# Graph attention and routed experts on one core: sends in every planner step, and the setup in short parts on three engines

## The chip, the core and the metric

The kernel runs on one NeuronCore of a Trainium2 chip. The core has TensorE (PE, matrix products; PEld is its weight load), VectorE (DVE), ScalarE (ACT), GpSimd (POOL) and SyncE (SP, which issues most of the DMAs). Each engine works through its own instructions in the order in which the program lists them, and waits at an instruction until what that one needs is there. The metric is the device time of one execution in microseconds, the median of the runs.

## The reference

The input `x` holds 64 batches of 256 rows with 256 features. Two layers follow each other. Each is an attention over a fixed graph of 256 nodes and then a per-row network, both added to the row.

```python
x = x + _L0_gnn_ref(_layernorm(x), adj, L0_gnn_W, L0_gnn_a)            # 4 heads of 64, elu
x = x + _L0_ffn_ref(_layernorm(x), L0_ffn_weight, L0_ffn_bias)          # one 256x256 linear layer
x = x + _L1_gnn_ref(_layernorm(x), adj, L1_gnn_W, L1_gnn_a)            # 1 head of 256, relu
x = x + _L1_ffn_ref(_layernorm(x), router_w, w1, b1, w2, b2)            # 8 experts, the best 2 per row
```

The attention: `h = x @ W`; `e[i,j] = leaky(h[i].a_src + h[j].a_dst)`, masked by `adj`; the output is `softmax(e) @ h`. The experts: `logits = tokens @ router_w.T`; the two largest per row get softmax weights; the output is `tokens + sum over the two of weight * (gelu(tokens @ w1[e]) @ w2[e] + b2[e])`. All of it is float32.

## The kernel before

**Tiles.** A batch is two tiles of 128 rows. The layers of one batch are one Python generator, `batch_layers` (line 485), that emits a stretch of instructions, yields a rank, and goes on in the next step: transposed input (116), statistics of the rows (353 to 362, the last two on GpSimd), projection `pq` (384), its exponentials (392) and scaling (400), the scores `z` (454, 461), `pv` (475), the linear layer `pf` (529), the second attention (419, 443, 475, 551), the normed rows `xng` and the residual `base` (569, 574), and the router logits (599).

**Planner.** The loop at line 1059 runs in steps. In each step every active generator is advanced once, by rising rank; the order in which instructions are emitted is the order in which each engine runs them. Three steps make a tick (`TICKS`), and `phase = step % 3`. One batch begins in each tick, at phase 2.

**Routed experts.** The first 62 batches are routed. They form chunks (`CHUNKS`: twelve of four batches, six of two, two of one). When a chunk has its logits, `route` (907) picks the two experts per row, counts positions with two small products (924, 925), computes the destinations, and then sends each row, by indirect DMAs from GpSimd (`send`, 888), to an area `xs` in device memory that is sorted by expert. A chunk of four batches has eight groups of two sends, one group at a time with a `yield` between. `later(rank, phases)` (901) yields until the step has one of the given phases. When all are sent, the pairs of 128-row tiles that are now full are appended to `waiting`, together with the names of the chunk's sends, on which the pairs' loads must wait (`needs`).

**Pairs.** `expert_pair` (710) handles one pair of 128 rows for one expert: loads `xr`, `xt` (726, 737) and the expert's weights `we` (752) by SP, a transposition on DVE (757), the two products `ph` (784) and `py` (799), the result `y` on DVE (809), its scaling on ACT (777), and two scattering indirect DMAs from GpSimd that add into `out` (`scatter`, 814). There are 131 pairs. Each scatter waits until both scatters of the pair before have landed (`before = added[-2:]`), since rows may repeat from pair to pair. Results have nine buffers. The planner begins waiting pairs at phase 1, as far as `credit` reaches (1072): it grows by 2 a tick (by 3 from step 180 on, `DRAIN_AT`) and is capped at 3. From step 209 on (`QUIET`) it begins one a step. One scatter is emitted per step. Batches 62 and 63 are not routed: all eight experts run on them (`dense_expert`, 836).

**Setup.** Before the first batch the kernel loads `adj`, makes the first mask (`fill_mask`, 145, on DVE and PE), and prepares the first layer's weights (`gnn_weights`, `score_columns`, `center`): four products and four reductions on DVE give the columns for the scores, and the columns' means are subtracted. Four more preparations, `prepare_f`, `prepare1`, the second mask and `prepare_r`, are jobs of one step each, begun one a step from step 3 on, and after them eight jobs that pack the experts' weights. Their DVE instructions stand between those of the first batches.

Of the kernel before, what the change touches and what calls it, by code (L numbers as in the profile page):

```python
# [27 lines left out]
def kernel(  # L28
# [102 lines left out]
    ones = const.tile([P, P], F32, tag="ones", name="ones")  # L131
# [3 lines left out]
    mhalf = const.tile([P, 2 * NT], F32, tag="mhalf", name="mhalf")  # L135
    nc.vector.memset(mhalf, -0.5)

    adj_i = work.tile([P, NT, N], adj.dtype, tag="z", name="adj_i", bufs=6)
    nc.scalar.dma_start(out=adj_i, in_=adj.rearrange("(t p) j -> p t j", p=P))

    masks = [
        const.tile([P, NT, N], F32, tag=f"mask{layer}", name=f"mask{layer}") for layer in range(2)
    ]

    def fill_mask(layer, op):
        mf = work.tile([P, NT, N], F32, tag="xT", name=f"maskf{layer}", bufs=4)
        nc.vector.tensor_scalar(mf, adj_i, 0.0, None, op0=op)
        pm = bank("pm", [NT, N])
        for t in range(NT):
            for j in range(NT):  # L150
                nc.tensor.transpose(
                    pm[:, j, t * P : (t + 1) * P], mf[:, t, j * P : (j + 1) * P], ident
                )
        nc.vector.tensor_copy(masks[layer], pm)

    fill_mask(0, ALU.is_gt)

    def center(w, cols):


        pc = bank("pc", [cols])
        for k in range(KT):
            nc.tensor.matmul(pc, mean_w, w[:, k, :], start=(k == 0), stop=(k == KT - 1))
        for k in range(KT):
            nc.vector.tensor_sub(w[:, k, :], w[:, k, :], pc)

    def gnn_weights(w, a, heads, slope, name):

        rows = lambda w, k: (
            w.rearrange("(p k) o -> k p o", k=KT) if heads > 1
            else w.rearrange("(k p) o -> k p o", k=KT)
        )[k]
        d = D // heads
        wx = const.tile([P, KT, heads, d + 3], F32, tag=name, name=name)  # L180
        for k in range(KT):
            nc.sync.dma_start(
                out=wx[:, k, :, :d],
                in_=rows(w, k).rearrange("p (h d) -> p h d", h=heads),
            )
        av = work.tile([P, 2, d], F32, tag="e", name=name + "_a", bufs=1)
        nc.scalar.dma_start(out=av.rearrange("p s d -> p (s d)"), in_=rows_to_all(a, 2 * d))
        flat = wx.rearrange("p k h c -> p k (h c)")
        return flat, lambda: score_columns(wx, av, heads, slope, name)

    def score_columns(wx, av, heads, slope, name):
        d = D // heads
        flat = wx.rearrange("p k h c -> p k (h c)")
        prod = work.tile([P, heads, d], F32, tag="hp", name=name + "_p", bufs=1)
        for k in range(KT):
            for s, c in ((0, d + 1), (1, d)):
                nc.vector.tensor_mul(
                    prod, wx[:, k, :, :d], av[:, s : s + 1, :].to_broadcast([P, heads, d])
                )
                nc.vector.tensor_reduce(wx[:, k, :, c : c + 1], prod, AX.X, ALU.add)  # L200
            nc.vector.tensor_scalar(
                wx[:, k, :, d + 1 : d + 2], wx[:, k, :, d + 1 : d + 2], 1.0 - slope, None,
                op0=ALU.mult,
            )
            nc.vector.tensor_scalar(
                wx[:, k, :, d + 2 : d + 3], wx[:, k, :, d : d + 1], slope - 1.0, None,
                op0=ALU.mult,
            )
        center(flat, heads * (d + 3))

    wx0, prepare0 = gnn_weights(w0, a0, H, SLOPE0, "wx0")
    xblk = {0: load_blocks(0)}
    xin = {0: load_batch(0)}
    prepare0()
    wx1, prepare1 = gnn_weights(w1g, a1g, 1, SLOPE1, "wx1")

    wf_in = work.tile([P, KT, D], F32, tag="xT", name="wf_in", bufs=4)
# [3 lines left out]
    wfT = const.tile([P, KT, D], F32, tag="wfT", name="wfT")  # L221
# [3 lines left out]
    def prepare_f():  # L225
        pw = bank("pw", [KT, D])
        for t in range(KT):
            for k in range(KT):
                nc.tensor.transpose(
                    pw[:, k, t * P : (t + 1) * P], wf_in[:, t, k * P : (k + 1) * P], ident  # L230
                )
        nc.vector.tensor_copy(wfT, pw)
        center(wfT, D)

        nc.vector.tensor_scalar(bias_f, bias_f, -1.0, None, op0=ALU.add)

    r_in = work.tile([E, D], F32, tag="x1b", name="r_in", bufs=1)
    nc.scalar.dma_start(out=r_in, in_=router)
    rT = const.tile([P, KT, E], F32, tag="rT", name="rT")

# [58 lines left out]
    def once(work):  # L299
        work()  # L300
        return
        yield


    setup = [
        lambda work=work: once(work)
        for work in (prepare_f, prepare1, lambda: fill_mask(1, ALU.not_equal), prepare_r)
    ]
    setup += [lambda e=e: pack_expert(e) for e in range(E)] + [fill_spare]

# [590 lines left out]
    def later(rank, *phases):  # L901

        yield rank
        while more and order_steps[-1] % TICKS not in phases:
            yield rank

    def route(c, row0, nt, n, last, xng, lg):
# [11 lines left out]
        spread = nt == NTC  # L919
# [42 lines left out]
        if last:  # L962
            ends_at = rt([E], "ends_at", 2, I32)
            vec.tensor_copy(ends_at, rows[0])
        yield from later(95, 1, 2)
        mark = len(sent)
        for t in range(nt):
            for k in range(2):
                send(xng[t // NT][:, t % NT, :], pos[:, k, t : t + 1])
            if n and spread and t in (1, 3):  # L970
                ids, ef = next(parts) or (None, None)
            if not last:
                yield from later(95, 1, 2)
            elif t % 2:
                yield 95
        needs = sent[mark:]
# [77 lines left out]


    DRAIN_AT, QUIET = TICKS * (B - 4), TICKS * B + 17
    SETUP_AT = 3
    with tc.manual_schedule():
        while more or active or waiting or dense_jobs or scatters:
            phase = step % TICKS  # L1060
            if phase == 2 and more:
                nxt = next(batches, None)
                more = nxt is not None
                if more:
                    begin(nxt, 25)
            if step >= SETUP_AT and setup:
                begin(setup.pop(0)(), 90)
            if step >= QUIET:
                if waiting and len(scatters) < 3:
                    begin(waiting.pop(0)(), 90)  # L1070
            elif phase == 1:
                credit = min(credit + (2.0 if step < DRAIN_AT else 3.0), 3.0)
                while waiting and credit >= 1.0:
                    credit -= 1.0
                    begin(waiting.pop(0)(), 90)
            if dense_jobs and step % DENSE == 0:
                begin(dense_jobs.pop(0)(), 90)
# [54 lines left out]
```

## Time and profile before

| | |
|---|---|
| Median of 3 runs | 1650.05 us (1646.56 to 1652.72) |
| Profiled execution | 1651.53 us, of which the span that the profile covers is 1649.6 |
| Busy in the span | PE 1476.3 us (89%), PE weight load 1299.8, DVE 1323.8 (80%), ACT 831.0 (50%), POOL 889.4 (54%) |
| Mean granted PE clock | 0.955 |
| Scatters (line 820, POOL) | 262, 1585 ns each |
| Sends (line 890, POOL) | 248, 1012 ns each |
| Chain that ended last | PE 62%, DVE 21%, DMA 5%, POOL 4% |

A busy share is an average over the whole span. The parts of this kernel have different limits, so the prediction reads it in parts: the start, the ticks of the middle, and the end. In a row of a timeline the first number is the start in us from the beginning of the span, the second the duration; `[... <-X]` is the idle time of the engine before the instruction and what ended it.

### The profile page before, as it was taken

Reading aid. Unit: us, or ns where it says so; the run is one execution under the profiler, and the core shown is the slowest. Engines: PE = TensorE matmul, PEld = TensorE weight load, DVE = VectorE, ACT = ScalarE, POOL = GpSimd, SP = SyncE. Lnnn points to the kernel's source line nnn. Section 1 sums busy time; section 2 is a strip of 40 time slices with the busy share of each in tenths; the row PEclk is TensorE's granted clock in tenths of the full one; section 3 lists DMA queues with packets and bytes.
Section 4 is the critical chain, followed back from the end, with each engine's and each line's share of the span. In section 5 each row is a group of like instructions: output and inputs, shape, how many; then the busy total and the mean of one; then the engine's idle time right before and its main releaser. Section 6 shows DMA issues by size and latency. Waiting matters only on the chain.

```text
span 1649.6 us, 30216 instructions
## 1 busy us (share of the span) xinstructions
PE 1476.3 (89%) x8474; PEld 1299.8 (79%) x8474; DVE 1323.8 (80%) x4494; ACT 831.0 (50%) x1832; POOL 889.4 (54%) x853
## 2 busy tenths in 40 slices
PE   5898888999999999999999999999989997599930
PEld 4777777778888888888888888887878886488820
DVE  6888989999898989898989898999988877545510
ACT  0244344445666666565656666655555565343310
POOL 0121343444757575756575757566664677544444
PEclk8999999999999999999999999999999998799965
DMA  4812123254756565656666675756575667887633
GB/s 109 231 44 58 55 71 101 72 140 113 158 132 135 135 146 135 140 138 145 140 127 156 117 170 108 163 117 146 135 140 124 136 127 152 188 178 135 128 38 45
DMA packets 364132, 207.37 MB, mean 126 GB/s; under 512 B 264248, under 2 KB 334912, under 8 KB 363968
## 3 DMA queue, kind: packets, MB, share of 16 engines
q1 hardware_dynamic: 313344, 137.07, 33.7%
q0 software_dynamic: 49632, 67.39, 22.8%
q8 instruction: 70, 1.15, 0.3%
q10 hardware_dynamic: 992, 0.99, 0.2%
q14 instruction: 94, 0.77, 0.2%
HBM read 116.19 MB, written 89.15 MB: 124 GB/s over the span
## 4 chain that ended last, share of the span: by engine, by line
PE 62%; DVE 21%; DMA 5%; POOL 4%; issue 3%; ACT 3%; SPq 1%; DVEq 0%; POOLq 0%; ACTq 0%
PE pv L475 14%; PE ph L784 13%; PE py L799 12%; PE pq L384 5%; PE pq L419 5%; PE pf L529 4%; DVE z L461 3%; PE pt L368 3%; DVE stats L353 3%; DMA out_dram<-y,xt 3%; POOL out_dram L820 2%; PE pl L599 2%; DVE mv L354 2%; ACT xT L374 1%; PE pd L454 1%
## 5 line engine op out<-in xcount | busy, mean ns | idle before, releaser
L820 POOL DMA_INDIRECT out_dram<-y,xt x262 | 415.4, 1585 | 241.1 <-DMA out_dram<-y,xt 87.6
L475 PE MATMUL pv<-q,z 128*128 128x65 f32 (+1 forms) x2560 | 368.5, 299 | 3.7 <-DVE z L461 3.7
L475 PEld LDWEIGHTS pv<-q,z 128*128 128x128 f32 x2560 | 331.5, 194 | 15.5 <-DVE z L461 4.0
L361 POOL TENSOR_SCALAR rstd<-mv 128x4 f32<-128x4 f32 (+1 forms) x132 | 71.0, 538 | 432.2 <-DVE mv L354 337.1
L890 POOL DMA_INDIRECT xs<-xng,pos x248 | 250.9, 1012 | 68.8 <-issue 65.7
L799 PE MATMUL py<-w2s,hT 128*128 (+1 forms) x1176 | 266.1, 379 | 1.3 <-ACT hT L790 1.2
L784 PE MATMUL ph<-sT,we 128*128 128x256 f32 x1048 | 242.8, 385 | 11.8 <-DVE y L809 9.6
L799 PEld LDWEIGHTS py<-w2s,hT 128*128 128x128 f32 x1176 | 219.5, 190 | 30.0 <-ACT hT L790 2.2
L374 ACT COPY xT<-pt 128x512 f32<-128x512 f32 x192 | 113.3, 590 | 232.5 <-PE pt L368 232.4
L784 PEld LDWEIGHTS ph<-sT,we 128*128 128x128 f32 x1048 | 198.9, 194 | 38.5 <-issue 9.9
L461 DVE SCALAR_TENSOR_TENSOR z<-pd,q,mask 128x256 f32<-128x256 f32 x512 | 211.1, 473 | 0.3 <-PE pd L454 0.2
L790 ACT ACTIVATE hT<-ph,we 128x256 f32<-128x256 f32 x294 | 122.5, 472 | 126.2 <-PE ph L784 103.8
L362 POOL TENSOR_TENSOR rstd<-rstd,mhalf 128x4 f32<-128x4 f32 (+1 forms) x132 | 163.0, 1235 | 11.0
L777 ACT ACTIVATE y<-y,w 128x256 f32<-128x256 f32 x262 | 112.6, 501 | 100.1 <-DVE y L809 100.1
L353 DVE BATCH_NORM_STATS2 stats<-x 128x6 f32<-128x256 f32 x384 | 156.3, 407 | 2.2
L384 PE MATMUL pq<-wx,xT 128*128 128x268 f32 x512 | 139.2, 418 | 8.6 <-DVE wt L257 4.2
L419 PE MATMUL pq<-wx,xT 128*128 128x259 f32 x512 | 129.1, 394 | 15.6 <-ACT xT L374 15.6
L809 DVE TENSOR_TENSOR y<-py,b2s 128x512 f32<-128x512 f32 x131 | 85.8, 686 | 68.6 <-PE py L799 48.8
L384 PEld LDWEIGHTS pq<-wx,xT 128*128 128x128 f32 x512 | 101.8, 204 | 30.4 <-issue 6.9
L419 PEld LDWEIGHTS pq<-wx,xT 128*128 128x128 f32 x512 | 91.9, 189 | 42.0 <-ACT xT L374 30.7
L529 PE MATMUL pf<-wfT,xT 128*128 128x256 f32 x512 | 124.1, 386 | 0.0
L551 ACT ACTIVATE rel<-pv,rinv 128x256 f32<-128x256 f32 x128 | 53.9, 474 | 110.6 <-DVE rinv L482 110.5
(152 smaller groups left out, 2256.1 us busy)
## 6 DMA issues: line engine op xcount, KB each, us to landing
we<-wpack SPq DMA_DIRECT2D x139, 288.0 KB
xr<-xs SPq DMA_DIRECT2D x524, 64.0 KB
xblk<-in_x_dram SPq DMA_DIRECT2D x256, 64.0 KB
xin<-in_x_dram SPq DMA_DIRECT2D x64, 256.0 KB
out_dram<-base SPq DMA_DIRECT2D x64, 256.0 KB
out_dram<-y,xt POOLq DMA_INDIRECT x262, 3.9
xs<-xng,pos POOLq DMA_INDIRECT x248, 2.9
xs<-fill SPq DMA_DIRECT2D x9, 260.0 KB
```

Of the source, the lines that this page charges most:

```text
L353: nc.vector.bn_stats(stats[:, t, :], src[:, t, :])
L362: nc.gpsimd.tensor_tensor(rstd[:, :n], rstd[:, :n], mhalf[:, :n], ALU.pow)
L374: nc.scalar.copy(dst, pt)
L384: nc.tensor.matmul(pq.rearrange("p h c -> p (h c)"), xT[:, k, t * P : (t + 1) * P], wx[:, k, :], start=(k == 0), stop=(k == KT - 1),)
L419: nc.tensor.matmul(pq, xT[:, k, t * P : (t + 1) * P], wx1[:, k, :], start=(k == 0), stop=(k == KT - 1),)
L461: nc.vector.scalar_tensor_tensor(z[:, j, :], pd[:, i, :], q[:, j, h, d + 2 : d + 3], mask[:, j, :], op0=ALU.max, op1=ALU.mult,)
L475: nc.tensor.matmul(pv[:, h, :], z[:, j, t * P : (t + 1) * P], q[:, j, h, : d + 1], start=(j == 0), stop=(j == NT - 1),)
L529: nc.tensor.matmul(pf[:, t, :], xT[:, k, t * P : (t + 1) * P], wfT[:, k, :], start=(k == 0), stop=(k == KT - 1),)
L784: nc.tensor.matmul(ph[:, f, :], we[:, k * D + f * P : k * D + (f + 1) * P], xT[:, k, :], start=(k == 0), stop=(k == KT - 1),)
L799: nc.tensor.matmul(py[:, t, :], hT[:, f, t * P : (t + 1) * P], w2s[:, e, f * D : (f + 1) * D].rearrange("p e c -> p (e c)"), start=(f == 0 ...
L820: d = nc.gpsimd.indirect_dma_start(out=out_rows, out_offset=bass.IndirectOffsetOnAxis(ap=xt[:, t, 0:1].bitcast(I32), axis=0), in_=y[:, t, ...
L890: d = nc.gpsimd.indirect_dma_start(out=xs_d[: E * CAP * PAIR, :], out_offset=bass.IndirectOffsetOnAxis(ap=at, axis=0), in_=xe, in_offset=None,
```

## The change

It has four parts.

1. In `route`, the sends yield plainly: one group of two sends is emitted in every step, where `later` kept them to phases 1 and 2. The second half of the allotment of pairs (`next(parts)`) moves from the fourth group to the fifth, which is the same step as before.
2. The credit of pairs fills up in each tick to 2 (3 from `DRAIN_AT` on) and is no longer saved from one tick to the next.
3. The columns for the scores are made with fewer, wider instructions: the scores vector is scaled first, the products for the source and destination columns go to one tile, and one reduction takes both. Of the first layer's products one half is made by GpSimd, of the second layer's all. The copies of both masks and of `wfT` out of PSUM move from DVE to ACT. `adj` is loaded after the first scores vector instead of before it, and the first mask is made after the first layer's columns. A one-element exponential on ACT stands ahead of the rest and takes the table load.
4. The preparations are generators with a yield between their parts, so that a part is emitted per step; they begin at step 4, and with them the packing of the experts begins one step later. Some temporary tiles use other buffers.

```diff
-        nc.vector.tensor_copy(masks[layer], pm)
-
-    fill_mask(0, ALU.is_gt)
+        nc.scalar.copy(masks[layer], pm)
...
-        prod = work.tile([P, heads, d], F32, tag="hp", name=name + "_p", bufs=1)
+        nc.vector.tensor_scalar(av[:, 0, :], av[:, 0, :], 1.0 - slope, None, op0=ALU.mult)
+        prods = []
         for k in range(KT):
-            for s, c in ((0, d + 1), (1, d)):
-                nc.vector.tensor_mul(
-                    prod, wx[:, k, :, :d], av[:, s : s + 1, :].to_broadcast([P, heads, d])
-                )
-                nc.vector.tensor_reduce(wx[:, k, :, c : c + 1], prod, AX.X, ALU.add)
...
+            eng = nc.vector if heads > 1 and k == 0 else nc.gpsimd
...
+            for i, part in enumerate((1, 0)):
+                eng.tensor_tensor(
+                    prod[:, i], wx[:, k, :, :d],
+                    av[:, part : part + 1, :].to_broadcast([P, heads, d]), ALU.mult,
+                )
+            prods.append(prod)
+        yield 90
+        for k, prod in enumerate(prods):
+            nc.vector.tensor_reduce(
+                wx[:, k, :, d : d + 2].rearrange("p h c -> p c h"), prod, AX.X, ALU.add
+            )
...
+    warm = small.tile([P, 1], F32, tag="warm", name="warm", bufs=1)
+    nc.scalar.activation(warm, ones[:, :1], AF.Exp)
+    for _ in fill_mask(0, ALU.is_gt):
+        pass
...
-        nc.vector.tensor_copy(wfT, pw)
-        center(wfT, D)
+        yield 5
+        nc.scalar.copy(wfT, pw)
+        yield 90
+        yield from center(wfT, D)
...
-        yield from later(95, 1, 2)
+        yield 95
         mark = len(sent)
         for t in range(nt):
             for k in range(2):
                 send(xng[t // NT][:, t % NT, :], pos[:, k, t : t + 1])
-            if n and spread and t in (1, 3):
+            if n and spread and t in (1, 4):
                 ids, ef = next(parts) or (None, None)
             if not last:
-                yield from later(95, 1, 2)
+                yield 95
...
-    SETUP_AT = 3
+    SETUP_AT = 4
...
-                credit = min(credit + (2.0 if step < DRAIN_AT else 3.0), 3.0)
+                credit = min(credit + 3.0, 2.0 if step < DRAIN_AT else 3.0)
```

More of the change, by code (lines that the diff above doesn't have):

```diff
@@ L136 @@
     nc.vector.memset(mhalf, -0.5)
-    adj_i = work.tile([P, NT, N], adj.dtype, tag="z", name="adj_i", bufs=6)
-    nc.scalar.dma_start(out=adj_i, in_=adj.rearrange("(t p) j -> p t j", p=P))
     masks = [
@@ L185, in gnn_weights @@
             )
-        av = work.tile([P, 2, d], F32, tag="e", name=name + "_a", bufs=1)
+        av = work.tile([P, 2, d], F32, tag="e" if heads > 1 else "x2", name=name + "_a",
+            bufs=1 if heads > 1 else 4)
         nc.scalar.dma_start(out=av.rearrange("p s d -> p (s d)"), in_=rows_to_all(a, 2 * d))
@@ L193, in score_columns @@
         flat = wx.rearrange("p k h c -> p k (h c)")
-        prod = work.tile([P, heads, d], F32, tag="hp", name=name + "_p", bufs=1)
+        nc.vector.tensor_scalar(av[:, 0, :], av[:, 0, :], 1.0 - slope, None, op0=ALU.mult)
+        prods = []
         for k in range(KT):
-            for s, c in ((0, d + 1), (1, d)):
-                nc.vector.tensor_mul(
-                    prod, wx[:, k, :, :d], av[:, s : s + 1, :].to_broadcast([P, heads, d])
-                )
-                nc.vector.tensor_reduce(wx[:, k, :, c : c + 1], prod, AX.X, ALU.add)
-            nc.vector.tensor_scalar(
-                wx[:, k, :, d + 1 : d + 2], wx[:, k, :, d + 1 : d + 2], 1.0 - slope, None,
-                op0=ALU.mult,
+            eng = nc.vector if heads > 1 and k == 0 else nc.gpsimd
+            prod = work.tile(
+                [P, 2, heads, d], F32, tag=("hp", "x1", "rel", "base")[k + (0 if heads > 1 else KT)],
+                name=f"{name}_p{k}", bufs=2 if heads == 1 and k else 1,
+            )
[3 more added lines that the diff above has]
+                    av[:, part : part + 1, :].to_broadcast([P, heads, d]), ALU.mult,
+                )
+            prods.append(prod)
+        yield 90
+        for k, prod in enumerate(prods):
+            nc.vector.tensor_reduce(
+                wx[:, k, :, d : d + 2].rearrange("p h c -> p c h"), prod, AX.X, ALU.add
             )
+        for k in range(KT):
             nc.vector.tensor_scalar(
@@ L208, in score_columns @@
             )
-        center(flat, heads * (d + 3))
+        yield 90
+        yield from center(flat, heads * (d + 3))
     wx0, prepare0 = gnn_weights(w0, a0, H, SLOPE0, "wx0")
+    adj_i = io.tile([P, NT, N], adj.dtype, tag="xr", name="adj_i", bufs=5)
+    nc.scalar.dma_start(out=adj_i, in_=adj.rearrange("(t p) j -> p t j", p=P))
     xblk = {0: load_blocks(0)}
     xin = {0: load_batch(0)}
-    prepare0()
+    for _ in prepare0():
+        pass
+    warm = small.tile([P, 1], F32, tag="warm", name="warm", bufs=1)
+    nc.scalar.activation(warm, ones[:, :1], AF.Exp)
+    for _ in fill_mask(0, ALU.is_gt):
+        pass
     wx1, prepare1 = gnn_weights(w1g, a1g, 1, SLOPE1, "wx1")
@@ L231, in prepare_f @@
                 )
-        nc.vector.tensor_copy(wfT, pw)
-        center(wfT, D)
+        yield 5
+        nc.scalar.copy(wfT, pw)
+        yield 90
+        yield from center(wfT, D)
         nc.vector.tensor_scalar(bias_f, bias_f, -1.0, None, op0=ALU.add)
-    r_in = work.tile([E, D], F32, tag="x1b", name="r_in", bufs=1)
+    r_in = work.tile([E, D], F32, tag="base", name="r_in")
     nc.scalar.dma_start(out=r_in, in_=router)
@@ L305 @@
     setup = [
-        lambda work=work: once(work)
-        for work in (prepare_f, prepare1, lambda: fill_mask(1, ALU.not_equal), prepare_r)
+        prepare_f, prepare1, lambda: fill_mask(1, ALU.not_equal), lambda: once(prepare_r)
     ]
```

## The prediction

> **What bounds the kernel now.** I read the slices first, then busy time by windows, the chain that ended last, ticks cut out between successive `pq` matmuls of line 384, and the timeline of the first 45 us. Three regimes appear.
>
> The slices (page, part 2) give the outline: busy tenths, 41.2 us each.
>
> ```profile
> PE   5898888999999999999999999999989997599930
> POOL 0121343444757575756575757566664677544444
> ```
>
> PE fills the middle, not the first seven slices, and is empty in the last one while POOL is not. Busy time in three stretches of the end (start:end, length, then busy us by engine with counts):
>
> ```profile
> 1500.00:1550.00 50.00, 50.00 (x233) 44.01 (x232) 26.40 (x61) 18.24 (x43) 21.66 (x15) 1.00 0.79 147
> 1550.00:1600.00 50.00, 30.90 (x144) 26.86 (x142) 14.89 (x36) 14.67 (x34) 21.85 (x14) 0.83 0.41 57
> 1600.00:1650.00 50.00, 0.00 (x0) 0.00 (x0) 0.00 (x0) 0.00 (x0) 21.60 (x14) 0.50 0.34 42
> ```
>
> PE, DVE and ACT have nothing left after 1600; POOL issues 14 scatters. The chain that ended last says why:
>
> ```profile
> 1628.43 0.30 issue
> 1628.74 3.64 DMA out_dram<-y,xt
> 1632.51 0.71 issue
> 1633.21 1.54 POOL out_dram L820
> 1634.76 0.30 issue
> 1635.06 3.78 DMA out_dram<-y,xt
> 1638.97 0.71 issue
> 1639.68 1.54 POOL out_dram L820
> ```
>
> A pair's two scatters wait until the pair before has landed, so pairs leave one per 6.42 us (1581.90 to 1639.68 is nine of them). The pair whose scatter starts at 1428.18 is the 101st of 131; the 30 after it set the end. The tail is a count of pairs not yet scattered when the batches run out.
>
> The middle goes by ticks of three planner steps. Around the first full chunk of pairs:
>
> ```profile
> 299.34:315.38 16.04, 14.59 (x96) 12.71 (x96) 14.90 (x49) 5.69 (x14) 5.23 (x7) 1.00 0.20 58
> 315.38:333.72 18.34, 15.46 (x94) 12.60 (x95) 16.26 (x57) 7.22 (x18) 10.74 (x12) 1.00 0.36 87
> 333.72:351.24 17.52, 16.29 (x94) 13.90 (x95) 15.77 (x57) 7.34 (x18) 7.43 (x10) 0.90 0.43 99
> 351.24:376.63 25.39, 24.94 (x147) 22.34 (x147) 24.18 (x86) 17.51 (x40) 9.58 (x12) 1.00 0.58 164
> 376.63:398.01 21.38, 21.14 (x128) 18.92 (x128) 19.75 (x63) 12.94 (x28) 9.42 (x11) 1.00 0.45 116
> 419.34:437.21 17.87, 17.63 (x111) 15.82 (x110) 14.23 (x46) 9.08 (x18) 13.37 (x14) 1.00 0.75 147
> ```
>
> The first three hold no expert pair and PE has room; then come 3, 2, (2,) 1 pairs, and PE is full. A pair costs 3.46 us there (21.33 less 17.87). The start, finally:
>
> ```profile
> 16.92 1.28 ACT L392 ACT_TABLE_LOAD   x1 [16.92 <-PE pq L384]
> 18.52 0.88 DVE L400 SCALAR_TENSOR_TENSOR q<-pq,rstd,q 128x256 f32<-128x256 f32 x2 [2.05 <-ACT q L392]
> ```
>
> The table load stands in front of batch 0's first scaling, and after it DVE does 5.1 us for the second layer's columns (19.31 to 23.2, subtraction at 24.49) before the first `z` at 25.35.
>
> [...]here the second scatter of a pair takes 3.64 to 3.80 us from trigger to landing[...]. [...]granted 0.80 from 1375 to 1425, where PE idles 9.33 and 6.59 us at a time[...].[...]
>
> **The change, part by part.** The sum is made against the profiled execution, 1651.53 us around a span of 1649.6; that is 1.48 above the median 1650.05.
>
> *Sends.* A chunk of four batches makes 8 groups of two sends. Before, groups run in phases 1 and 2 only, so 8 take 12 steps; now 8. Chunk two sends from step 46 in both: its pairs were listed at step 58 and begun at 61, now listed at 54 and begun at 55. With credit capped at 2, a chunk's eight pairs begin 2,2,2,2 a tick, where they began 3,2,2,1. Followed to the end, 111 pairs have begun by step 208 before and 114 after, and the planner ends at step 235, not 238. From step 209 to the end the scatters stand one a step, so three fewer lie in the tail: 3 x 6.42 = **-19.3 us**. It is less if the dense experts, not the chain, held those steps: from 1442 to 1562 PE is full at 6.9 us a pair plus a dense half, and scatters come every 7.4; the lag behind PE grows all through it (the last result is ready at 1589.2, the last scatter starts at 1639.7), so the chain governs.
>
> *What these pairs cost earlier.* They land in ticks that had none. The tick of 16.41 us (step 46 to 49) gets one: PE 14.62+3.46=18.1, +1.8. The tick of 21.21 loses it; DVE's 19.78 less 1.75, the gaps kept, -0.8. The ticks of 18.34 and 17.52 get two each and become PE-full at 21.4: +3.1 and +3.9. 25.39 goes from three pairs to two: 22.0, -3.4. 17.87 goes from one to two: +3.5. Sum **+8** (5 to 11).
>
> *Steady cycles.* Before: 25.18+21.38+21.33+17.87 = 85.8 for eight pairs, PE idle 1.0 of it. After, four ticks near 21.4; but the tick with the routing arithmetic keeps it: DVE 23.5-1.75 = 21.75 busy (result 0.69, turning 0.70, weights 0.35 per pair), and where DVE bounds a tick it is 97% busy (14.03 of 15.55 less a 1.07 wait), so 22.4 against PE's 21.5. DVE's next ticks need 20.6 of 21.4 and win this back; PE waits only as far as its lead on DVE is under a microsecond. The lead is about 5 us for `z` (ready 631.75, used 636.6), less where a copy feeds PE at once. I take +0.2 a cycle for nine cycles, **+2** (-5 to +9).
>
> *POOL.* A third send group per tick adds 2 x 1.3 us between the statistics of phase 0 and the scatter. There POOL had 1.55 us waiting for the scatter before, and 2.91 idle after it (574.01 and 580.42): 4.46 of room for 2.6, so nothing. Behind those sends stand the scatter, then the next `rstd`, for which ACT's exponentials wait. SP: the loads of a chunk's first pairs wait for its last send, issued two steps earlier now and five before. In the trace a send issued at 566.2 would land by 571 (landings take 4 to 5 us) and SP comes to its next loads at 571.9: just in time; what is queued behind on SP is prefetch.
>
> *Start.* The scores vector goes first on ACT's queue, 0.53 us earlier: DVE starts at 5.3. DVE: scale 0.17, two products 0.42 each, mask 0.43, two reductions of double width at an estimated 0.75, small ones 0.3: 8.7. GpSimd makes the other two products meanwhile. No row shows that operation there[...]. The floor is 0.54 (its 128x520 memset)[...]. Then column means 1.26, subtraction 0.75, projection 2.47: 13.2. The table load now runs on an idle ACT: exponentials 0.44, scaling to 14.6, where it was 19.4. The mask and `wfT` copies leave DVE (0.68, 0.66, 0.69) for an ACT that is idle there (0.59 for that size). DVE's list from the first `z` (15.7) to the first finished `x1b` adds up to 12.8[...]: 29.5, against 40.4. I take **-11** (-6 to -14: weight loads from 31 on could delay later steps). The one-step later packing of experts is far ahead of its first use and costs nothing; adj, moved behind the vector, is needed 0.5 us later, under the products.
>
> *Drain.* Routing stands on the same steps; step 199 begins two pairs instead of three where PE idles anyway, and two DVE-heavy ticks hold one pair more: **+1**.
>
> Sum: -19.3+8+2-11+1 = -19.3; 1651.5 becomes 1632, and against the median about **1630**.
>
> **Rivals.** *Small gain:* the drain sticks to the last routing (PE idle 9 us at a time from 1380 to 1442 speaks for it), the fewer scatters merely start later, and the tail keeps its length less 5: 1645. Against it: after 1577 only scatters remain. *DVE bounds the routing tick:* no lead, +1.5 to 2 per cycle, +15: 1643. For it: 21.75 busy against 21.4; against it: two light ticks follow. *Larger gain:* the start gives 14 and four scatters' time leaves the tail (26 remain where 30 did), early pairs cost 5: 1614. *Slower:* POOL. If sends in front of the scatter, or landings slowed by their traffic, take more than the 4.46 us of room, the next `rstd` is late and DVE with it, in three of four ticks of 40: 1 us of excess is +30, 1660. It decides from 1.9 us above my 2.6. Against it: POOL is 54% busy and now has fewer runs of five scatters in consecutive steps. *The change not doing what it says:* excluded for order, as sends do stand in each step and three steps go.
>
> **Numbers.** Measurement tells about 0.5%, 8.25 us. Forecast (1620 to 1640) 0.6, larger gain 0.13, DVE bound 0.1, small gain 0.12, slower 0.05. Faster than 1641.8: 0.6+0.13, half of DVE bound and a third of small gain, 0.82; slower than 1658.3: 0.05; same 0.13. Range 1612 to 1645: it leaves out the slower case, half of the small gain and the far end of the larger one, about 0.17.
>
> **What would show it.** First scaling near 14.6 and third `pq` near 31; ticks from step 58 on of 21 to 22 us, with no 25 or 18; last PE work to last scatter still some 60 us, at 6.4 a pair, with 26 scatters after step 207. It is wrong if routing ticks stay at 23 or more, if POOL's `rstd` has no idle time before it in each tick, or if SP's pair loads wait on sends.

## The result, and the profile after

The kernel after takes 1622.96 us (median of 4 runs, 1618.62 to 1626.77), the kernel before 1649.59 beside it: ratio 0.9838, 95% interval 0.9805 to 0.9871. The forecast was 1630. The profiled execution of after has a span of 1616.8 us, 32.8 less than the span of before; why that is more than the 26.6 us between the medians is told below.

The slices of after, 40.4 us each (page, part 2):

```profile
PE   6898889899999999999999999999999999579970
POOL 2221435255766666575757575756765567744444
```

The outline is that of before: PE fills the middle, and the last slice is still empty of PE while POOL works. The end of after in three windows (start:end, length, then busy us by engine with counts in the order PE, PEld, DVE, ACT, POOL; then clock, DMA share, GB/s):

```profile
1500.00:1550.00 50.00, 50.00 (x234) 44.01 (x233) 25.47 (x57) 18.23 (x43) 23.16 (x15) 1.00 0.67 121
1550.00:1600.00 50.00, 16.54 (x77) 14.22 (x75) 8.11 (x20) 7.89 (x18) 23.12 (x15) 0.69 0.39 48
1600.00:1650.00 50.00, 0.00 (x0) 0.00 (x0) 0.00 (x0) 0.00 (x0) 6.17 (x4) 0.81 0.11 16
```

The last 50 us window holds four scatters where it held fourteen. The chain that ended last is of the same make as before, a pair's landing and then the next pair:

```profile
1600.52 1.54 POOL out_dram L841
1602.06 0.30 issue
1602.37 3.77 DMA out_dram<-y,xt
...
1606.27 0.71 issue
1606.98 1.54 POOL out_dram L841
```

1606.98 less 1600.52 is 6.46 us. The ticks around the first full chunk of pairs, cut between `pq` matmuls (line 384, now 405):

```profile
291.27:308.46 17.19, 16.82 (x96) 14.42 (x96) 13.97 (x47) 3.27 (x9) 3.41 (x5) 0.86 0.44 112
308.46:333.15 24.69, 22.81 (x127) 20.17 (x127) 23.11 (x85) 16.58 (x37) 7.55 (x10) 0.93 0.38 100
333.15:354.48 21.33, 21.09 (x127) 18.87 (x126) 18.99 (x61) 11.94 (x26) 12.41 (x14) 1.00 0.54 135
440.26:462.00 21.74, 21.50 (x132) 19.27 (x130) 19.27 (x64) 13.37 (x30) 16.11 (x16) 1.00 0.68 151
```

After one tick of 24.69 every tick to the 57th is 21.3 to 21.7 us long, and DVE is busy for at most 19.8 us of one. The start of after, from the timelines of ACT, DVE and POOL:

```profile
1.68 1.28 ACT L232 ACT_TABLE_LOAD   x1 [1.68 <-PEq L1135]
...
7.01 1.31 POOL L205 TENSOR_TENSOR wx_p<-wx,wx_a 128x256 f32<-128x256 f32 x2 [5.27 <-DMA wx<-in_L_gnn_W_dram]
...
14.13 0.48 DVE L421 SCALAR_TENSOR_TENSOR q<-pq,rstd,q 128x256 f32<-128x256 f32 x1 [1.46 <-ACT q L413]
```

The scaling of batch 0 begins at 14.13 us (18.52 before). Its first tile is done at 14.61 and its second at 16.07; in before both are done at 19.40. The third `pq` is at 31.42 (42.81).

**Where the time went.** A batch's first `pq` is a good milestone, since each batch has exactly one. The stretches between some of them, in us, with the number of pairs that are scattered whole between the 64th `pq` and the end. "Last scatter" is the first of the last pair's two. "Setup" and "sends" tell which part of the change a kernel holds; the rows below the second are the experiments of the next section.

| Kernel | to 5th | 5 to 15 | 15 to 25 | 25 to 57 | 57 to 64 | 64th to last scatter | span |
|---|---|---|---|---|---|---|---|
| before | 72.34 | 171.82 | 193.05 | 688.31 | 176.02 | 338.14 (46) | 1649.6 |
| after | 61.20 | 172.33 | 206.73 | 686.59 | 171.95 | 308.18 (42) | 1616.8 |
| setup alone | 62.25 | 171.94 | 192.96 | 688.18 | 174.26 | 332.62 (46) | 1632.4 |
| sends alone | 73.66 | 171.72 | 206.60 | 686.60 | 172.65 | 312.68 (42) | 1633.9 |
| parts at once | 73.27 | 171.11 | 206.69 | 686.57 | 176.27 | 315.29 (42) | 1639.3 |
| two a tick to the end | 62.16 | 172.35 | 206.73 | 686.57 | 162.08 | 328.65 (44) | 1628.5 |
| one dense batch | 63.81 | 172.21 | 206.68 | 686.62 | 172.16 | 323.73 (44) | 1635.4 |
| one dense expert | 65.68 | 172.25 | 206.70 | 686.53 | 172.28 | 304.98 (42) | 1618.2 |
| three dense batches | 62.59 | 172.01 | 206.68 | 686.56 | 171.88 | 296.48 (40) | 1606.4 |

From before to after: -11.1, +0.5, +13.7, -1.7, -4.1, -30.0, and -0.1 behind the last scatter: -32.8.

### The profile page after: what moved, and what is told of

It reads as the page before. It is cut to its first block, busy times and chain, and to the rows that moved or that the text cites. A ratio compares the mean times of both kernels' runs of the same rounds, so it can differ in the third digit from the quotient of the medians.

```text
span 1616.8 us, 30207 instructions
## 1 busy us (share of the span) xinstructions
PE 1472.5 (91%) x8474; PEld 1299.6 (80%) x8474; DVE 1317.2 (81%) x4479; ACT 833.5 (52%) x1840; POOL 892.6 (55%) x859
## 4 chain that ended last, share of the span: by engine, by line
PE 65%; DVE 22%; DMA 3%; issue 3%; POOL 3%; ACT 2%; SPq 1%; DVEq 0%; POOLq 0%; ACTq 0%
PE pv L496 15%; PE ph L805 14%; PE py L820 13%; PE pq L405 6%; PE pq L440 5%; PE pf L550 4%; DVE z L482 4%; PE pt L389 4%; DVE stats L374 3%; PE pl L620 2%; DMA out_dram<-y,xt 2%; DVE mv L375 2%; ACT xT L395 1%; POOL out_dram L841 1%; DVE x L556 1%
## 5 line engine op out<-in xcount | busy, mean ns | idle before, releaser
L382 POOL TENSOR_SCALAR rstd<-mv 128x4 f32<-128x4 f32 (+1 forms) x132 | 59.6, 452 | 435.3 <-DVE mv L375 357.5
L405 PEld LDWEIGHTS pq<-wx,xT 128*128 128x128 f32 x512 | 100.2, 200 | 31.4 <-issue 8.4
L375 DVE BATCH_NORM_AGGREGATE mv<-stats 128x2 f32<-128x6 f32 x512 | 93.1, 182 | 17.5
```

Of the source, the lines that this page charges most:

```text
L405: nc.tensor.matmul(pq.rearrange("p h c -> p (h c)"), xT[:, k, t * P : (t + 1) * P], wx[:, k, :], start=(k == 0), stop=(k == KT - 1),)
```

## The experiments

Line numbers are those of the kernel after. Ratios are to the kernel before, run on the same chip.

**The two halves of the change.** The first kernel has the setup of after and the sends and the credit of before; the second is the reverse.

```diff
-        yield 95
+        yield from later(95, 1, 2)
         mark = len(sent)
...
-                credit = min(credit + 3.0, 2.0 if step < DRAIN_AT else 3.0)
+                credit = min(credit + (2.0 if step < DRAIN_AT else 3.0), 3.0)
```

> The kernel before with the setup of the kernel after (scores vector first, products shared with GpSimd, copies on ScalarE, table load early), sends and credit as before. My theory: the start ends about 11 us earlier (third pq at 31.4 us, 42.8 before), every later tick keeps its length, the tail keeps its 30 scatters after step 207 and 211.5 us; the span is 1638 to 1640 and the ratio to before about 0.993. Rival, the gain is swallowed where the kernel becomes full: the third pq is at 31.4 but the 64th is at 1298 or later, and the ratio is 0.998 to 1.0.

Measured: 1636.37 us, ratio 0.9943 (0.9929 to 0.9957). The third `pq` is at 31.79, the 64th at 1289.59, 12 us before that of the kernel before: the gain of the start is carried to the end whole. The tail has its 30 scatters after step 207, in 206.1 us.

> The kernel before with the sends in every step and the credit capped at 2, setup as before. My theory after reading the trace of after: no gain before the tail (64th pq at about 1309, 1301.5 before), then 26 scatters after step 207 in about 182 us instead of 30 in 211.5; the span is 1625 to 1630, the ratio 0.986 to 0.989, and with the run that has the setup alone it adds up to the whole change. Rival, the two parts work only together (the earlier start is what makes room for the early pairs): the two ratios add up to less than 60% of the whole gain.

Measured: 1628.01 us, ratio 0.9887 (0.9844 to 0.993). The 64th `pq` is at 1311.23, later than in before, and the 26 scatters after step 207 take 183.6 us. The two gains, 0.57% and 1.13%, add up to 1.70% where both together have 1.62%: no dependence between the halves shows, and about a third of the gain is the setup's.

**The credit.** The kernel after with the credit line of before (the second hunk above, alone).

> The kernel after with the credit of before (up to 3 saved, 2 added a tick), so that the eight pairs of a chunk begin 3, 2, 2, 1 again; the planner leaves the same 26 scatters after step 207. If pairs cost the same wherever they stand (3.46 us each in a full tick), ticks of 25, 21.4, 21.4 and 18 come back, four ticks still last 85.8 us, and the time is that of after within 3 us (ratio to before 0.980 to 0.987). If even spreading is what gained, each cycle is longer by 0.5 us or more and the ratio is above 0.988.

Measured: 1620.70 us, ratio 0.986 (0.9813 to 0.9908). The ticks of 17.9 and 24.8 are back, the stretch from the 25th to the 57th `pq` is 686.57 us (686.59 in after), and from the 5th `pq` to the last scatter it takes 1547.2, after 1545.8. The credit moves pairs between ticks and gains nothing that these runs can tell; the gain of this half is the earlier listing.

**The number of pairs left at the end.** The kernel after with two pairs a tick to the last batch:

```diff
-                credit = min(credit + 3.0, 2.0 if step < DRAIN_AT else 3.0)
+                credit = min(credit + 3.0, 2.0)
```

> The kernel after with the credit kept at 2 pairs a tick to the last batch (3 a tick from step 180 in after), so that 32 scatters instead of 26 stand after step 207. Tail counted in pairs at 7.0 us each: the stretch from the scatter of step 207 to the last scatter is 224 us (181.5 in after), of which the ticks from step 181 on give back 15 to 30 us, since they hold fewer pairs: 12 to 28 us slower than after, ratio to before 0.990 to 1.002. Counted at 6.42 us each: the stretch is 39 longer instead of 42. Rival, the last routing or the matmuls set the end: the stretch grows by less than 15 us and the run is no slower than after.

Measured: 1628.91 us, ratio 0.990 (0.9854 to 0.9946). The 32 scatters after step 207 take 224.7 us, and that of step 207 stands at 1393.87, 31.6 us before that of after. By then eight pairs fewer had begun their first product on PE, about 4 us each, and six fewer had been scattered. So a pair left to the tail costs about 7 us there, and less is saved where it was taken away.

**What bounds the tail.** Two kernels take matmuls away from it. In the first, one batch at the end runs through all experts instead of two, which puts two more pairs in the routing; in the second, seven of the eight experts of both dense batches are left out.

```diff
-    CHUNKS = (4,) * 12 + (2,) * 6 + (1, 1)
+    CHUNKS = (4,) * 12 + (2,) * 6 + (1, 1, 1)
```

> The kernel after with one batch computed by all eight experts at the end instead of two: eight halves of expert work fewer on TensorE (8 x 3.46 = 27.7 us), and two more pairs with their scatters (133, 28 of them after step 207). If the scatter chain sets the end: 2 x 7.0 = 14 us more there, at most 4 back from calmer transfers: 8 to 16 us slower than after. If TensorE or the dense experts set the end: 27.7 less 2 x 3.46, some 20 us faster than after.

Measured: 1636.48 us, ratio 0.9929 (0.9905 to 0.9953): some 15 us slower than after, with 21 us less work for PE.

```diff
-            dense_jobs.extend(lambda e=e: dense_expert(e) for e in range(E))
+            dense_jobs.extend(lambda e=e: dense_expert(e) for e in range(E - 1, E))
```

> The kernel after with seven of the eight experts of the two dense batches left out of the computation (14 halves of expert work, 48 us of TensorE, and seven loads of 288 KB, all after step 211). If the scatter chain sets the end: 26 scatters remain after step 207; they come at 6.4 to 6.9 us each instead of 7.0, since less is on the DMA engines, so 2 to 14 us faster than after. If TensorE sets the end: 30 to 48 us faster.

Measured: 1615.90 us, ratio 0.9809 (0.979 to 0.9828). Its windows at the end:

```profile
1500.00:1550.00 50.00, 31.28 (x106) 23.54 (x104) 11.00 (x27) 11.40 (x28) 21.94 (x15) 0.83 0.53 85
1550.00:1600.00 50.00, 0.00 (x0) 0.00 (x0) 0.82 (x2) 1.81 (x4) 24.67 (x16) 0.50 0.35 40
```

PE is done by 1549 and was 63% busy before that; POOL goes on with fifteen and sixteen instructions per window (fifteen in both in after). With 48 us of matmuls gone the stretch from the 64th `pq` is 3.2 us shorter. The chain of scatters sets the end, not TensorE. The dense experts and the pairs bring loads with them, and beside loads a scatter landed later; the landings, from the views of `out_dram` in after between 1440 and 1480 and between 1565 and 1605:

```profile
DMA to landing us min/median/max: 3.7/5.0/5.3
...
DMA to landing us min/median/max: 3.7/3.8/3.8
```

The first is amid the pairs' loads (DMA share 0.79 from 1450 to 1500), the second when they have stopped (0.36 from 1565 to 1605). In the two stretches between (1480 to 1520 and 1520 to 1560) the median is 4.3 and 3.7. In the median a landing was thus up to 1.2 us longer beside the loads, which could account for 7.0 instead of 6.4 us a pair; no run takes the loads alone away.

**A version from this.** If a pair costs 7 us of chain and TensorE has 40 us to spare, a batch should be taken from the routing and given to all experts:

```diff
-    CHUNKS = (4,) * 12 + (2,) * 6 + (1, 1)
+    CHUNKS = (4,) * 12 + (2,) * 6 + (1,)
...
-    WBUFS, XBUFS, YBUFS = 7, 5, 9
+    WBUFS, XBUFS, YBUFS = 7, 5, 7
...
-        base = work.tile([P, NT, D], F32, tag="dbase" if dense else "base", name="base")
+        base = work.tile(
+            [P, NT, D], F32, tag="dbase" if dense else "base", name="base",
+            bufs=DENSE if dense else 2,
+        )
```

> The kernel after with three batches computed by all eight experts at the end instead of two (a third buffer for their base, two result buffers of pairs fewer to make room): two pairs fewer, 24 scatters after step 207, and 27.7 less 6.9, some 21 us more on TensorE, whose last matmul ends 44 us before the last scatter in after. If the scatter chain sets the end: 2 x 7.0, some 14 us faster than after (ratio to before about 0.975). If TensorE or the dense results set it as soon as they are added to: 0 to 15 us slower than after.

Measured: 1600.48 us, ratio 0.9715 (0.9689 to 0.974), 2.9% faster than before and about 20 us faster than after. Its last two windows and the last steps of its chain:

```profile
1500.00:1550.00 50.00, 50.00 (x234) 44.01 (x233) 25.25 (x58) 18.53 (x44) 21.73 (x14) 1.00 0.54 93
1550.00:1600.00 50.00, 40.65 (x179) 32.78 (x177) 20.91 (x46) 11.04 (x26) 25.02 (x16) 1.00 0.39 51
```

```profile
1586.81 1.74 PE ph L808 x8
...
1589.70 1.54 POOL out_dram L844
1591.24 0.30 issue
1591.55 3.82 DMA out_dram<-y,xt
1595.49 0.71 issue
1596.20 1.76 POOL out_dram L844
```

PE's last matmul ends at 1595.50 and the last pair's first scatter starts at 1596.20: they now nearly meet. The gain is more than the 14 us expected; the profile shows 11.7 of it in the stretch from the 64th `pq`, so part of the rest is the spread of single executions.

**An earlier drain.** Three pairs a tick from step 174 instead of 180 (`TICKS * (B - 6)`).

> The kernel after with three pairs a tick allowed from step 174, not 180: up to two pairs more have been scattered by each step from 184 to 200, and still 26 stand after step 207. If the scatters have been one unbroken chain since about step 188 (they come every 7.3 us from there to the end in after), two pairs fewer are left in it and the end comes 2 x 7.3 less 2 x 3.46, some 8 us sooner. If the last routing sets when the final 26 may start, nothing changes: within 3 us of after.

Measured: 1616.65 us, ratio 0.9808 (0.9783 to 0.9833), not told apart from after. In the trace the ticks from the 57th to the 64th `pq` are 6.6 us longer and the stretch to the last scatter 7.9 shorter, which is two pairs' price in a full tick (6.9) and one pair's in the tail (7.35): 41 scatters are left after the 64th `pq`, one less and not two.

**The ticks with the first pairs.** The kernel after without the second bias (a sum with zeros here), so that DVE does less for each pair:

```diff
-        nc.vector.tensor_add(y, py, b2s[:, e, :].to_broadcast([P, 2, D]))
-        return y
+        return y, py
...
-            nc.scalar.activation(y[:, t, :], y[:, t, :], AF.Copy, scale=w[:, t : t + 1])
+            nc.scalar.activation(y[:, t, :], py[:, t, :], AF.Copy, scale=w[:, t : t + 1])
```

> The kernel after with the addition of the experts' second bias left out (it is zero in these inputs), so that ScalarE scales a pair's result straight from PSUM and VectorE does 0.69 us less per pair. If VectorE was the bound of the first ticks with pairs (the 15th pq to the 25th, 206.7 us in after, 193.1 before), that stretch gets 4 to 9 us shorter; if TensorE was, it stays within 1 us. Full cycles of four ticks (85.8 us) are bound by TensorE and stay. The tail stays at 26 scatters in 180 to 184 us. Time: 4 to 9 us faster than after, or the same.

Measured: 1620.64 us, ratio 0.9841 (0.9811 to 0.9872). The stretch from the 15th to the 25th `pq` as one window in before, in after and in this kernel:

```profile
244.16:437.21 193.05, 180.89 (x1092) 158.14 (x1093) 176.35 (x601) 100.61 (x228) 95.16 (x105) 0.98 0.44 109
```

```profile
233.53:440.26 206.73, 194.59 (x1156) 171.42 (x1157) 185.49 (x628) 114.16 (x255) 108.76 (x113) 0.98 0.48 116
```

```profile
236.45:442.90 206.45, 194.81 (x1157) 171.64 (x1157) 179.54 (x617) 113.27 (x255) 108.88 (x113) 0.98 0.50 117
```

DVE has 6 us less to do and the time is the same to 0.3 us, so the results' share of DVE was not the bound. Thirteen pairs are done in this stretch instead of nine. PE is busy for 13.70 us more in after than in before, and the stretch is 13.68 us longer, so that PE's idle time is 12.1 to 12.2 us in both. The equal sums hide an exchange, which the windows of the single ticks show: in six of the ten ticks PE idles less than before, by 4.9 us together, and in one, from which the change took the pair away, it idles 4.9 us more. That tick in before and in after:

```profile
278.13:299.34 21.21, 20.03 (x115) 17.50 (x115) 19.78 (x71) 13.40 (x30) 9.58 (x12) 0.92 0.27 82
268.85:291.27 22.42, 16.34 (x99) 13.49 (x99) 19.20 (x69) 11.29 (x30) 15.01 (x16) 0.95 0.38 102
```

PE has a pair less to do, and the tick is longer. In it DVE waits for an exponential of ACT, and ACT for the row statistics of GpSimd (`rstd`), which stand behind four sends and the first pair's two scatters:

```profile
276.91 0.43 ACT L413 ACTIVATE q<-pq,rstd 128x12 f32<-128x12 f32 x2 [2.94 <-POOL rstd L383]
277.21 0.88 DVE L421 SCALAR_TENSOR_TENSOR q<-pq,rstd,q 128x256 f32<-128x256 f32 x2 [2.22 <-ACT q L413]
```

In before these two waits were 1.8 and 0.4 us. In the next tick, 96 matmuls in both kernels, the granted clock is 0.86 instead of 1.00, and PE is busy for 16.82 us instead of 14.59. In the tick of 24.69 us (24.70 in this kernel) the trace has no wait of DVE in either kernel: DVE is busy for 23.11 us with other work, and the first of the pairs' results comes behind it. So the run says nothing of that tick, and no run moves the scatter or DVE's other work out of these two ticks.

**The parts of the setup.** Three kernels, each the kernel after with one of them undone: the products all on DVE; no early exponential; and the four later preparations each issued whole in one step.

```diff
-            eng = nc.vector if heads > 1 and k == 0 else nc.gpsimd
+            eng = nc.vector
```

> The kernel after with the products of the score columns all on VectorE, none on GpSimd. VectorE gets two more of 0.38 us for the first layer, but no longer waits 0.64 us for GpSimd's: the first scaling (ends 14.6 in after) ends within 0.5 us of that. The second layer's four add 1.5 us on VectorE between 19 and 23 us: the third pq (31.42 in after) at 32 to 33. If GpSimd's share is what gained the start, the first scaling ends at 16 or later.

Measured (one run): 1622.03 us; first scaling begun at 15.25 (14.13 in after), third `pq` at 33.17 (31.42). In the other profiles with GpSimd's products and the parts the first scaling begins at 13.81 to 14.56, and where batch 0's `pq` takes as long as here (3.94 us; last section) the third `pq` is at 31.4 to 32.0. So the share of GpSimd gains 0.7 to 1.4 us at the first scaling and 1.1 to 1.8 at the third `pq`, by a single run; I had expected less than 0.5 at the first. The weights' subtraction begins no later than in the others (11.08; 10.49 to 11.24), but batch 0's transposition (0.71 us) and two small operations, which DVE did ahead of it in after, stand behind it in this kernel's order.

```diff
-    nc.scalar.activation(warm, ones[:, :1], AF.Exp)
+    nc.vector.memset(warm, 0.0)
```

> The kernel after without the early one-column exponential that loads ScalarE's table, so that the load comes with the first real use. If that is the exponential of the first batch, 1.28 us come back onto the path: the first scaling ends at 15.9 (14.6 in after) and the third pq is at 32.7. If the mask copy before it, on an idle ScalarE, loads the same table, nothing moves and the early load gained nothing by itself.

Measured (one run): 1623.49 us; ACT's timeline:

```profile
5.26 1.28 ACT L155 ACT_TABLE_LOAD   x1 [5.26 <-DMA wx<-in_L_gnn_W_dram]
10.14 0.59 ACT L155 COPY mask<-pm 128x512 f32<-128x512 f32 x1 [3.60 <-PE pm L152]
14.05 0.44 ACT L413 ACTIVATE q<-pq,rstd 128x12 f32<-128x12 f32 x2 [3.32 <-PE pw L249]
```

The load goes ahead of the mask copy, which is now ACT's, while ACT waits for its operand, and none stands before the exponentials. The first scaling begins at 14.36, within the 13.81 to 14.56 of the kernels that have the early exponential. The third `pq` is at 29.50, but that is no gain of leaving it out: batch 0's `pq` takes 2.08 us here and 3.94 in after (last section), and three kernels that have the early exponential and this shorter `pq` (2.08 to 2.16) have their third `pq` at 29.4 to 29.9. The early exponential gains nothing that shows once ACT copies the mask. One load of 1.28 us served the copies and the exponentials of this start.

```diff
-        prepare_f, prepare1, lambda: fill_mask(1, ALU.not_equal), lambda: once(prepare_r)
+        lambda job=job: once(lambda: list(job()))
+        for job in (prepare_f, prepare1, lambda: fill_mask(1, ALU.not_equal), lambda: once(prepare_r))
```

> The kernel after with the four later pieces of the setup (final-layer weights, second layer's columns, second mask, router) each issued whole in one planner step instead of in parts, one a step; the engines stay as in after. If the parts gained the start, VectorE stands waiting for GpSimd's products (1.9 us) and TensorE's column means between 17 and 31 us: the third pq at 34 to 37 us (29.4 to 31.9 in the runs of after's start). If the engines and the order of the loads gained it, the third pq stays at 32.5 or earlier. Later ticks and the tail are those of after: at most 0.3% of time either way.

Measured: 1637.50 us, ratio 0.9896 (0.9864 to 0.9929), the ratio of the sends alone. First scaling as in after (14.41 begun), but the second `pq` is at 31.42 and the third at 43.50, later than in the kernel before. PE's timeline:

```profile
18.01 0.60 PE L476 MATMUL pd<-ident,q 128*128 128x128 f32 x4
24.42 2.10 PE L162 MATMUL pc<-wx,mean_w 128*128 128x259 f32 x4 [5.82 <-DVE wx L216]
26.31 1.06 PE L476 MATMUL pd<-ident,q 128*128 128x128 f32 x4
30.51 1.11 PE L152 MATMUL pm<-ident,maskf 128*128 128x128 f32 x4 [3.14 <-DVE maskf L147]
```

The scores of batch 0 (the second `pd`) and the second batch stand in PE's order behind column means for which PE waits 5.82 us, and behind a mask for which it waits 3.14; DVE in its turn waits 1.94 and 2.06 us for PE's means. So the start's gain past the first scaling needs the parts. Shared engines without parts gave 4.1 us at the first scaling (14.41 begun, 18.52 before) and had lost them by the fifth `pq` (73.27, 72.34 before). Of these 4.1 us the runs give 0.7 to 1.4 to GpSimd's products and none to the early exponential; the wider instructions, the order of the loads and the mask's place were not undone one by one. The expectation had 34 to 37 us for the third `pq` and 0.3% of time; it was 43.5 and 0.6%.

## Why the prediction was right, and where not

The time was inside the forecast's own range (1620 to 1640) and 7 us under its value, as errors of both signs left 13.5 us in the profile (-32.8 where the sum had -19.3).

- **Start, -11: right.** Measured -11.1 to the fifth `pq` (9.8 over all the profiles, see below), and the third `pq` near the time named. Of the first scaling only one tile was done at 14.6, the other at 16.07, as batch 0's `pq` took 3.94 us where the sum had 2.47; in the four profiles where it took 2.08 to 2.16 both tiles are done at 14.7 to 15.2. The working credited it to DVE's shorter list and the moved copies and load. The runs show that the order by parts decides it: without the parts the shorter list gains nothing by the fifth `pq`. GpSimd's products took 0.64 to 0.71 us each, and the sum had no wait for them: DVE waited 0.64 us for the first two.
- **Early pairs, +8: the size was off, +13.7.** From the tick of 17.52 on the ticks came within 0.3 us of the working. The miss lies in the five ticks before it, which got 10.1 us longer where the sum had 4.1, and two steps failed there. "The tick of 21.21 loses it, -0.8" took 22.42: the working kept DVE's gaps, but DVE waited 2.2 us where it had waited 0.4, PE idled for 6.1 us, and the tick behind it, at a granted clock of 0.86, took 1.2 us more for the same work. And the tick of 18.34, from step 58 to 61, did not become "PE-full at 21.4": it took 24.69, with DVE busy for 23.11 and without a wait, so "no 25" did not hold for it. The other ticks' idle time was room, as the working had it.
- **Steady cycles, +2: measured -1.7** from the 25th to the 57th `pq`. A cycle of four ticks took 85.77 us in both; the difference lies mainly in two ticks of before, of 18.45 and 19.44 us where their like took 17.88. DVE is busy for at most 19.8 us of a tick, so the rival that had DVE bound the routing tick fell here.
- **Drain, +1: measured -4.1** between the 57th and the 64th `pq` (-1.8 with the setup alone, -3.4 with the sends alone). It is the difference of a few ticks of 21 to 31 us, and its cause was not tested.
- **Tail, -19.3: right in kind, the size -30.0.** "Three fewer" counted the planner's steps (238 to 235) and pairs begun, and "6.42" was read where nothing but scatters runs. What counts is the scatters still to come from where one stands in nearly every step, about the 64th `pq`: 42 instead of 46, and 7.35 us each (338.14 by 46; 308.18 by 42); longer landings amid the pairs' loads (5.0 us in the median, 3.8 when they have stopped) may be a part of that. Four times 7.35 is 29.4. The text itself named 26 scatters after step 207 where 30 did, and the larger gain among its rivals took four; its sum did not. The last matmul to the last scatter was to stay some 60 us; it is 40.4, mainly because a pair less takes 3.5 us from PE and 7.35 from the chain, which is 15.6 us for four.
- **POOL and SP.** "Nothing" for POOL held in the steady cycles: between 440 and 620 it waits for DVE 39.6 us in total before the statistics, and ACT never waits for them (8.8 us in before). It did not hold in the tick of 22.42 us above, where sends and scatters stood in front of `rstd` and DVE waited with it: what the slower rival had for most ticks happened once. SP was to be just in time and was not:

```profile
SPq L747 <- DMA xs<-xng,pos: 22.2, 5, 5.8
```

In the same window of the waits of after (total us, times, longest), SP's pair loads wait for sends. Landings of 4 to 5 us were the author's estimate; between 440 and 620 a send landed after 2.9 us in the median in before (2.4 to 6.4) and after 3.1 in after (2.5 to 5.5). What is queued behind is loaded ahead of need, and the ticks stay at 21.3 to 21.7, so no cost of it shows.

The rivals: a small gain through the last routing is refuted by the tail's stretch, which follows the count of scatters in nine kernels; slower through POOL did not come about beyond that one tick. The larger gain, 1614, had its mechanism right in the tail, but not that early pairs cost only 5.

**Span and median.** The span fell by 32.8 us, the median by 26.6. The profiled execution of after is the fastest of its four (1618.62). From the third to the fourth `pq` the profiled execution of after takes 14.1 us; the ten other profiles whose setup is in parts take 14.1 once and 16.4 to 20.0 else, the three without 15.5 to 16.2. In the profiles with parts the granted clock goes with it, 1.00 in those of 14.1 us and 0.50 for a part of the stretch in the others (last section). Over the fifth `pq` times of those eleven (59.6 to 66.0, mean 63.3) and of the three (72.3 to 73.7, mean 73.1) the start gains 9.8 us rather than 11.1. That covers a part of the difference; the rest is within the intervals.

## What to carry to other kernels

When the end of a kernel is a chain of transfers that each wait for the one before, count the links that remain when the chain fills up, and price a link where most of them stand, not in the quiet at the end, where it took 6.46 us here; then weigh each against what it costs to do it earlier, here 7.35 against 3.4 us. That comparison, once made, pointed to a larger gain than the change itself: moving work from the chain to an engine that idles beside it. In a prologue, an order in which no engine waits for a result asked for just before gained more than moving operations to idle engines, which without that order had gained nothing by the fifth batch (its first `pq` at 61.20 us in after, 73.27 without the parts, 72.34 in before). And idle time of the busiest engine is room for more work only in ticks that no other engine sets: here it was in most ticks, and in two, of 22.42 and 24.69 us, it was not.

## What the runs showed of the hardware

**The same instructions at half the clock in some executions.** The 32 `pv` matmuls of batch 1 in after, and in the kernel without the early exponential, which has the same work there (start, duration):

```profile
33.30 3.68 PE L496 MATMUL pv<-q,z 128*128 128x65 f32 x32
```

```profile
33.20 6.93 PE L496 MATMUL pv<-q,z 128*128 128x65 f32 x32
```

The granted clock from 31 to 38 us is 1.00 in the first and 0.50 in the second. From 24 to 31 us PE was busy for 3.98 and 3.97 us, but in the second the mean clock of that stretch is already 0.83: its record drops to 0.50 at 28.64. The first record stands at 1.00 from 16.13 to 46.85, which is 30.72 us, and then at 0.50 for 3.41; in the second the changes at 11.57, 28.64 and 42.30 are 17.07 and 13.66 apart, so that the stretches are nine, one, five and four times 3.41. Why the same half-idle work had two outcomes, no run here tests.

The times follow the record. With the setup in parts the stretch from the third to the fourth `pq` takes 14.1 us where the clock stays at 1.00, 16.4 to 16.5 where it is 0.50 for 6.8 us, 18.8 where it is so for 10.2, and 19.9 to 20.0 for 13.7. Earlier, batch 0's eight `pq` matmuls take 3.94 us in after and 2.08 in the kernel without the early exponential; the records show the full clock from 16.13 and from 11.57 on. Profiles of the first kind have the third `pq` at 31.4 to 32.0, or 33.2 without GpSimd's products, those of the second at 29.4 to 29.9. So a single profile of this start can be several us off.

**Landings beside loads and without them.** In after a scatter landed 3.8 us after its trigger in the median between 1565 and 1605, when the pairs' loads had stopped, and 5.0 beside them, between 1440 and 1480 (views of `out_dram` above). No run here splits the 1.2 us.
